# The last steps of each output group in an attention kernel: row sums added in halves ahead of the regrouping, output multiplied one unit sooner and stored two units sooner

## The chip, the core and the metric

The kernel runs on one core of a Trainium2 chip. The metric is the device time of one execution in microseconds (us). Three runs of the kernel before took 2331.0, 2331.13 and 2335.51 us; the median is 2331.13 us.

## What is computed

The input `x` has 4 images of 64 x 64 pixels with 256 channels. For each image three products with weights give q and k (128 channels) and v (256 channels). They are then read as rows of length N = 4096, with no transposition, and attention is computed over the 4096 columns:

```python
q = einsum('bwhc,cd->bwhd', x, Wq) + bq          # k, v alike
pq, pk, pv = (t.reshape(B, -1, N) for t in (q, k, v))
energy = einsum('bcn,bcm->bnm', pq, pk)
attention = softmax(energy, axis=-1)
out = einsum('bcm,bnm->bcn', pv, attention)
return gamma * out.reshape(B, W, H, C) + x
```

Everything is float32. The kernel splits each operand of a matrix product into three parts of lower precision and sums several products of them.

## The kernel before, in words

**Groups and units.** An image is worked off in 8 groups (`NG`) of 512 output columns (`NB`), a group in 16 units (`NU`) of 256 rows of the softmax sum. So there are 4 x 8 x 16 = 512 units, numbered n from 0 to 511; t = n % 16 is the unit's place in its group, and "the turn" is the unit with t = 15. A loop at the end of the fast part writes out, unit by unit, what each engine does; the order is by hand, and every engine runs its own list in order.

**One unit n** on TensorE: the first third of the energies of unit n + 2 (`cross`, L369), half of the weighted sums of unit n (`attend`, L443, into PSUM banks `a` and `b`), the rest of the energies of unit n + 2 (`energy`, L384), a piece of the next image's projections (`step`, L257 and L274), and the other half of the sums (L443). On ScalarE: a scaling of the energies in PSUM (L370), the exponential into `x` (L387), and the upper part `h` of it (L393). On VectorE, `halves(n + 1)`: the running sum `s` of the exponentials (L404), which has two halves of 512 columns, and the two lower parts `ld` (L419, L421). In the unit t = 0 there is no sum, as `x` itself becomes the new `s`. `load_k` (L356, on POOL's queue) loads the keys of unit n + 5.

**The next image** is prepared meanwhile. `step` makes q, k and v of two pixel blocks in each group: the forms of q and k on VectorE (L310) at t = 8 to 11, the forms of v on ScalarE (L155) and VectorE (L165) at t = 12 to 15. All four forms of a group, two of q and k, then two of v, use one tile tag `pf` with two buffers, so that the first form of v needs the stores of the first q/k form to have landed, and the second form of v those of the second. `store()` sends finished forms to DRAM (L338, on SP's queue): four stores for a q/k form, at t = 10 and t = 12, two for a v form, at t = 14 and t = 0. Two loads of x (L211, SP) follow at t = 13. In the last image there is nothing left to prepare. At the end of an image, from t = 3 of its last group to t = 2 of the next image's first group, `load_v` (L343, POOL) loads the new image's v, two transfers of 384 KB per unit.

**The end of a group** is `finish`, a generator. It is started at the turn, and `proceed()`, the last thing in each unit, takes each active one to its next `yield`. So the position of a `yield` says in which unit of the following group a step is issued:

| step of `finish` | queue or engine | unit of the following group |
|---|---|---|
| two stores of the halves of `s` to DRAM (`zd`, L469) | SP | the turn itself |
| eight loads of them, regrouped, into `y` (L474) | SP | 0 |
| the two parts of the output tile `o` added (L480) | VectorE | 3 |
| the sums: two reductions with a transposition between (L483 to L490), the reciprocal (L491), its store (`rd`, L492) | VectorE, SP | 6 |
| the reciprocals loaded onto all partitions (`r`, in `o`, L495) | SP | 7 |
| `o` multiplied by `r` (L498) | VectorE | 9 |
| the residual x added to `o` by an accumulating DMA (L502) | POOL | 10 |
| `o` stored to the output (L505) | SP | 13 |

`o` has one buffer. At the next turn `emptied` (L463 on ScalarE, L461 on VectorE) moves the PSUM banks into `o`, so it needs that last store to have landed, and the next group's first `attend` needs the PSUM bank that it empties. `y` lies in the buffer of the group's q. The last group of all doesn't use `finish`: `finish_last` does its end, and for it alone `whole()` in `halves` adds the two halves of `s` (L410).

Of the kernel before, what the change touches and what calls it, by code (L numbers as in the profile page):

```python
# [9 lines left out]
F32 = mybir.dt.float32  # L10
# [3 lines left out]
ALU = mybir.AluOpType  # L14
AX = mybir.AxisListType
# [5 lines left out]
def kernel(  # L21
# [36 lines left out]
    nc = tc.nc  # L58
    B, W, H, C = x.shape
    P = 128  # L60
# [21 lines left out]
    NB = 512  # L82
    NJ = NB // P
    NG = N // NB
    NU = NM // 2
    STEPS = NG * NU
# [14 lines left out]
    with ExitStack() as fast:  # L101
# [8 lines left out]
        dram = pool("dram", 2, space=DRAM)  # L110
# [4 lines left out]

        vall = qkv.tile([P, NU, 2, 3, C], F32R, tag="v", name="v")
        wf = qkv.tile([P, 2, 3, KC, C], F32R, tag="wf", name="wf")
        zd = dram.tile([B * NG, 2, P, NB], F32, tag="zd", name="zd", bufs=1)
        rd = dram.tile([B * NG, NB], F32, tag="rd", name="rd", bufs=1)
        xs4 = work.tile([P, 4, 2, XB], F32, tag="o", name="xs", bufs=1)  # L120
        raw = ppool.tile([P, 2, KC, C], F32, tag="x", name="raw")
# [223 lines left out]
        def q_tile(g, name, dtype=F32R):  # L345
            return work.tile([P, NJ, 3, P], dtype, tag=f"q{g % 2}", name=name, bufs=1)
# [49 lines left out]
        def halves(n):  # L396
            if n >= B * STEPS:
                return
            x, h = units[n]

            def summed():
                if n % NU:
                    s = now["s"]
                    nc.vector.tensor_tensor(s, s, x, ALU.add)  # L404
                else:
                    now["s"] = x

            def whole():
                s = now["sum"] = now["s"]
                nc.vector.tensor_tensor(s[:, 0, :], s[:, 0, :], s[:, 1, :], ALU.add)  # L410

            after = 0 < n < 5
            if not after:
                summed()
            if n == B * STEPS - 1:
                whole()
            ld = ppool.tile([P, 2, 2, NB], F32R, tag="ld", name=f"ld_{n}")
            l, d = ld[:, 0], ld[:, 1]
            nc.vector.tensor_tensor(l, x, h.bitcast(F32), ALU.subtract)  # L419

            nc.vector.scalar_tensor_tensor(  # L421
                d, h.bitcast(F32), 1.0 + E, x, ALU.mult, ALU.subtract
            )
            if n == 2:
                next(vs)
                next(vs, None)
            if after:
                summed()
            units[n] = h, l, d
# [35 lines left out]
        def finish(n, o, s):  # L465
            b, g = divmod(n, NG)
            r4 = rall[:, n, :]
            for i in range(2):
                nc.sync.dma_start(zd[n, i], s[:, i, :])  # L469
            yield  # L470
            y = q_tile(n, f"y_{n}", F32).rearrange("p j f a -> p (j f) a")
            for j in range(NJ):
                for i in range(2):
                    nc.sync.dma_start(  # L474
                        y[j * 32 : (j + 1) * 32, NJ * i : NJ * (i + 1)],
                        zd[n, i].rearrange("(a p) (j c) -> j p a c", p=32, j=NJ)[j],
                    )
            for _ in range(3):
                yield
            nc.vector.tensor_tensor(o[:, 0], o[:, 0], o[:, 1], ALU.add)  # L480
            for _ in range(3):
                yield
            nc.vector.tensor_reduce(  # L483
                y[:, 8].rearrange("p (f c) -> p c f", f=NJ),
                y[:, :8].rearrange("p a (c f) -> p c f a", f=NJ),
                AX.X,
                ALU.add,
            )
            nc.vector.transpose(y[:, 9], y[:, 8])
            nc.vector.tensor_reduce(r4, y[:, 9].rearrange("p (f c) -> p f c", f=NJ), AX.X, ALU.add)  # L490
            nc.vector.reciprocal(r4, r4)  # L491
            nc.sync.dma_start(rd[n, :].rearrange("(p j) -> p j", j=NJ), r4)  # L492
            yield
            r = o[:, 1, 0]
            nc.sync.dma_start(r, rd[n, :].partition_broadcast(P))  # L495
            yield
            yield
            nc.vector.tensor_tensor(  # L498
                o[:, 0], o[:, 0], r.unsqueeze(1).to_broadcast([P, 2, NB]), ALU.mult
            )  # L500
            yield
            nc.gpsimd.dma_start(o[:, 0], xg[b, g], accum_op=ALU.add)  # L502
            for _ in range(3):
                yield
            nc.sync.dma_start(og[b, g], o[:, 0])  # L505

        def inside(ok, r):
# [148 lines left out]
        for i in range(NI):  # L656
# [35 lines left out]
            if i in (7, 10):  # L692
                cross(i // 9)
            elif i in (8, 11):
                energy(i // 9)
            elif i in (9, 12):
                upper(i // 10)
            elif i == 14:
                halves(0)
# [4 lines left out]
        for n in range(B * STEPS):  # L704
# [15 lines left out]
            p = n - 2 + (n > 17)  # L720
# [16 lines left out]
            if turn:  # L737
                active.append(finish(n // NU, now["o"], now["s"]))
            if t == 0 and n and not late:
                emptied(n - 1, 1, done, vector=True)  # L740
            halves(n + 1)
            step(p, "dve")
            if final:
# [13 lines left out]
    NB = 512  # L757
    NG = N // NB
    NJ = NB // P
    NP = NM // 2  # L760
    with tc.If(nc.values_load(again[0:1, 0:1]) > 0), ExitStack() as general:
# [91 lines left out]
        for b in range(B):  # L853
# [16 lines left out]
            for g in range(NG):  # L870
                ps = []
                mx = work.tile([P, 2, NB], F32, tag="mx", name=f"gmx_{b}_{g}")
                for t in range(NP):
# [9 lines left out]
                    p = ppool.tile([P, 2, NB], F32, tag="p", name=f"gp_{b}_{g}_{t}")  # L883
# [54 lines left out]
                for s in range(2):  # L938
                    y = work.tile([P, NB], F32, tag="y", name=f"gy_{b}_{g}_{s}")
# [33 lines left out]
```

## Time and profile before

| | |
|---|---|
| median of three runs | 2331.13 us |
| the profiled execution | 2329.23 us |
| its span, first to last instruction | 2327.4 us |
| around the span | 1.8 us |
| granted TensorE clock | 0.998 |
| TensorE busy | 2309.6 us |
| VectorE busy | 2175.4 us |
| ScalarE busy | 1798.7 us |
| moved by DMA | 445.30 MB |

The span counts the time from the first to the last instruction of the profiled execution. An engine's busy time leaves out its waiting. In a row of the profile "L443 PE MATMUL a<-h,v" stands for line 443, the engine, the operation, the tile written and the tiles read; PE is TensorE, PEld its weight loads, DVE VectorE, ACT ScalarE, POOL GpSimd and SP SyncE, which only issues DMAs. In the table of waits the columns are who waited for whom, us in total, times, and the longest. In a timeline they are start, duration, what, and in brackets the idle time before it and what ended it. In a stretch of the windows view they are the stretch, its length, each engine's busy time and instructions, the granted clock, the mean busy share of the 16 DMA engines, and GB/s. In the table of DMA issues the last column is the median time from issue to landing.

### The profile page before, as it was taken

To read this page: it belongs to the slowest core of one execution; us is meant where nothing else is said; L and a number is where in the kernel's file an instruction comes from. 1 tells how busy PE (TensorE), PEld (TensorE's weight loads), DVE (VectorE), ACT (ScalarE), POOL (GpSimd) and SP (SyncE) were. 2 spreads that over 40 slices of the span, in tenths; PEclk is the share of its full clock that TensorE was granted. 3 is DMA by queue.
4 is the path that set the end of the run, shared out by engine and by line. 5 is a ranking of instruction groups with operands and counts; after the bars stand their busy time and mean duration, and the time that the engine had idled before them with its cause. 6 is when DMAs were issued, how large, how long until landed. Compare 5 with 4: busy or idle time off the path is not lost.

```text
span 2327.4 us, 31990 instructions
## 1 busy us (share of the span) xinstructions
PE 2309.6 (99%) x10758; PEld 1931.5 (83%) x10758; DVE 2175.4 (93%) x2175; ACT 1798.7 (77%) x2918; POOL 417.3 (18%) x716
## 2 busy tenths in 40 slices
PE   9999999999999999999999999999999999999998
PEld 9888888888888888888888888888888888888886
DVE  8999999999999999999999999999999999888988
ACT  7778777777777777777777777777787787888785
POOL 7111111111311111111132111111113111111110
PEclk9999999999999999999999999999999999999999
DMA  8557765577985776656798567755579755455553
GB/s 271 164 165 205 206 180 157 164 206 203 303 246 161 208 206 179 168 170 190 205 324 240 170 183 206 200 167 165 171 226 332 207 135 144 141 136 150 151 149 97
DMA packets 232190, 445.30 MB, mean 191 GB/s; under 512 B 27986, under 2 KB 109652, under 8 KB 232020
## 3 DMA queue, kind: packets, MB, share of 16 engines
q0 software_dynamic: 101120, 280.54, 45.4%
q1 hardware_dynamic: 130352, 162.38, 20.8%
q8 instruction: 88, 1.44, 0.3%
q14 instruction: 82, 0.67, 0.1%
q10 hardware_dynamic: 548, 0.26, 0.0%
HBM read 321.92 MB, written 120.39 MB: 190 GB/s over the span
## 4 chain that ended last, share of the span: by engine, by line
PE 96%; DMA 3%; DVE 0%; ACT 0%; issue 0%; POOL 0%; ACTq 0%
PE a L443 39%; PE e L384 19%; PE b L443 19%; PE e L369 10%; PE qv L257 5%; PE v L274 3%; DMA out_dram<-o 1%; PE xt L219 1%; DMA k<-kf 1%; DMA o<-in_x_dram 1%; DMA xs<-in_x_dram 0%; ACT qv L292 0%; ACT o L463 0%; DVE xf L165 0%; POOL v L343 0%
## 5 line engine op out<-in xcount | busy, mean ns | idle before, releaser
L387 ACT ACTIVATE x<-e 128x512 f32<-128x512 f32 x960 | 522.5, 596 | 323.1 <-PE e L384 323.0
L370 ACT ACTIVATE e<-e 128x512 f32<-128x512 f32 x1024 | 546.7, 571 | 134.8 <-PE e L369 134.8
L443 PE MATMUL a<-h,v 128*128 128x512 f32 x2048 | 633.7, 391 | 4.4 <-ACT o L463 4.4
L443 PE MATMUL a<-ld,v 128*128 128x512 f32 x2048 | 631.1, 389 | 0.0
L443 PE MATMUL b<-ld,v 128*128 128x512 f32 x2048 | 630.6, 389 | 0.0
L419 DVE TENSOR_TENSOR ld<-x,h 128x1024 fp32r<-128x1024 f32 x480 | 584.6, 1218 | 36.6 <-ACT h L393 23.8
L404 DVE TENSOR_TENSOR s<-s,x 128x1024 f32<-128x1024 f32 x480 | 584.2, 1217 | 35.5 <-ACT x L387 34.2
L356 POOL DMA_DIRECT2D k<-kf x512 | 272.5, 532 | 1846.7 <-PE e L384 1742.7
L421 DVE SCALAR_TENSOR_TENSOR ld<-h,x 128x1024 fp32r<-128x1024 f32 x480 | 583.9, 1216 | 0.0
L384 PE MATMUL e<-q,k 128*128 128x512 f32 x2048 | 547.7, 389 | 0.0
L393 ACT ACTIVATE h<-x 128x1024 fp32r<-128x1024 f32 x480 | 510.6, 1064 | 14.2
L443 PEld LDWEIGHTS b<-ld,v 128*128 128x128 f32 x2048 | 384.2, 188 | 80.8 <-DVE ld L421 0.6
L443 PEld LDWEIGHTS a<-ld,v 128*128 128x128 f32 x2048 | 384.3, 188 | 80.6
L384 PEld LDWEIGHTS e<-q,k 128*128 128x128 f32 x2048 | 384.2, 188 | 79.8
L443 PEld LDWEIGHTS a<-h,v 128*128 128x128 f32 x2048 | 379.4, 188 | 79.4 <-ACT o L463 5.3
L369 PE MATMUL e<-q,k 128*128 128x512 f32 x1024 | 315.8, 390 | 2.1 <-DMA k<-kf 2.1
L369 PEld LDWEIGHTS e<-q,k 128*128 128x128 f32 x1024 | 191.6, 188 | 43.1 <-ACT h L393 1.4
L310 DVE SCALAR_TENSOR_TENSOR f<-f,qv 128x512 fp32r<-128x512 f32 x128 | 85.4, 678 | 0.3
L419 DVE TENSOR_TENSOR ld<-s,h 128x1024 fp32r<-128x1024 f32 x32 | 39.3, 1227 | 46.6 <-ACT h L393 46.6
L257 PE MATMUL qv<-wf,xf 128*128 128x256 f32 x576 | 77.2, 285 | 0.4 <-DVE qv L285 0.2
L257 PEld LDWEIGHTS qv<-wf,xf 128*128 128x128 f32 x576 | 73.7, 191 | 3.5 <-issue 0.5
L165 DVE SCALAR_TENSOR_TENSOR vf<-vf,v 128x512 fp32r<-128x512 f32 x96 | 65.2, 679 | 0.3 <-ACT vf L155 0.3
(90 smaller groups left out, 1129.3 us busy)
## 6 DMA issues: line engine op xcount, KB each, us to landing
k<-kf POOLq DMA_DIRECT2D x512, 384.0 KB, 3.6
vf<-vf SPq DMA_DIRECT2D x96, 384.0 KB, 5.3
v<-vf POOLq DMA_DIRECT2D x96, 384.0 KB, 8.8
kf<-f SPq DMA_DIRECT2D x128, 192.0 KB, 3.8
qd<-f SPq DMA_DIRECT2D x124, 192.0 KB, 3.8
q<-qd POOLq DMA_DIRECT2D x31, 768.0 KB, 5.8
zd<-s SPq DMA_DIRECT2D x62, 256.0 KB, 4.9
y<-zd SPq DMA_DIRECT2D x248, 64.0 KB, 4.2
```

Source lines behind the costliest of these rows:

```text
L257: nc.tensor.matmul(to[:, s, :], left, right.rearrange("p s a -> p (s a)") if w else right, start=(f == 2 and s == k == 0), stop=(f == 1 an ...
L310: nc.vector.scalar_tensor_tensor(f[:, :, :, j, :], h.bitcast(F32), s, y, ALU.mult, op)
L356: nc.gpsimd.dma_start(t, kf[b, u % NU])
L369: nc.tensor.matmul(e, *forms(n, i, 2), start=True, stop=False, skip_group_check=True)
L370: nc.scalar.mul(e, e, -REST)
L384: nc.tensor.matmul(e, *forms(n, i, f), start=False, stop=(f == 1), skip_group_check=True)
L387: nc.scalar.activation(x[:, i, :], e, AF.Exp, scale=(1.0 + E) ** 3 / E)
L393: nc.scalar.activation(h, units[n], AF.Identity, scale=UPPER)
L404: nc.vector.tensor_tensor(s, s, x, ALU.add)
L419: nc.vector.tensor_tensor(l, x, h.bitcast(F32), ALU.subtract)
L421: nc.vector.scalar_tensor_tensor(d, h.bitcast(F32), 1.0 + E, x, ALU.mult, ALU.subtract)
L443: nc.tensor.matmul(to, vall[:, t, i, f, j * P : (j + 1) * P], units[n][f][:, i, :], start=(t == 0 and i == 0 and f != 1), stop=(t == NU - ...
```

## The change

For every group, not only the last, `whole()` adds the two halves of `s` into the first, in `halves` for t = 15, which VectorE does in the unit t = 14. `finish` then stores one half, 256 KB in place of 512, and loads it back in four transfers of 64 KB in place of eight; the first reduction goes over 4 blocks in place of 8. One `yield` is taken out ahead of the multiplication and one ahead of the store: the multiplication is issued in unit 8, the residual add in unit 9, the output store in unit 11. On SP the output store thus stands ahead of the four stores of the second q/k form (t = 12) and of the two loads of x (t = 13), where it stood behind them. On POOL the residual add stands one unit's loads earlier.

```diff
-            if n == B * STEPS - 1:
+            if n % NU == NU - 1:
                 whole()
...
-            for i in range(2):
-                nc.sync.dma_start(zd[n, i], s[:, i, :])
+            nc.sync.dma_start(zd[n], s[:, 0, :])
             yield
             y = q_tile(n, f"y_{n}", F32).rearrange("p j f a -> p (j f) a")
             for j in range(NJ):
-                for i in range(2):
-                    nc.sync.dma_start(
-                        y[j * 32 : (j + 1) * 32, NJ * i : NJ * (i + 1)],
-                        zd[n, i].rearrange("(a p) (j c) -> j p a c", p=32, j=NJ)[j],
-                    )
+                nc.sync.dma_start(
+                    y[j * 32 : (j + 1) * 32, :NJ],
+                    zd[n].rearrange("(a p) (j c) -> j p a c", p=32, j=NJ)[j],
+                )
...
             nc.vector.tensor_reduce(
-                y[:, 8].rearrange("p (f c) -> p c f", f=NJ),
-                y[:, :8].rearrange("p a (c f) -> p c f a", f=NJ),
+                y[:, 4].rearrange("p (f c) -> p c f", f=NJ),
+                y[:, :NJ].rearrange("p a (c f) -> p c f a", f=NJ),
                 AX.X,
                 ALU.add,
             )
...
             nc.sync.dma_start(r, rd[n, :].partition_broadcast(P))
-            yield
             yield
             nc.vector.tensor_tensor(
                 o[:, 0], o[:, 0], r.unsqueeze(1).to_broadcast([P, 2, NB]), ALU.mult
             )
             yield
             nc.gpsimd.dma_start(o[:, 0], xg[b, g], accum_op=ALU.add)
-            for _ in range(3):
-                yield
+            yield
+            yield
             nc.sync.dma_start(og[b, g], o[:, 0])
```

More of the change, by code (lines that the diff above doesn't have):

```diff
@@ L117 @@
         wf = qkv.tile([P, 2, 3, KC, C], F32R, tag="wf", name="wf")
-        zd = dram.tile([B * NG, 2, P, NB], F32, tag="zd", name="zd", bufs=1)
+        zd = dram.tile([B * NG, P, NB], F32, tag="zd", name="zd", bufs=1)
         rd = dram.tile([B * NG, NB], F32, tag="rd", name="rd", bufs=1)
@@ L488, in finish @@
             )
-            nc.vector.transpose(y[:, 9], y[:, 8])
-            nc.vector.tensor_reduce(r4, y[:, 9].rearrange("p (f c) -> p f c", f=NJ), AX.X, ALU.add)
+            nc.vector.transpose(y[:, 5], y[:, 4])
+            nc.vector.tensor_reduce(r4, y[:, 5].rearrange("p (f c) -> p f c", f=NJ), AX.X, ALU.add)
             nc.vector.reciprocal(r4, r4)
```

## The prediction

> **What bounds the kernel now.** I read the page's busy shares first, then the waits of TensorE, then the waits of all engines, then the chain and the timeline at the places that those named.
>
> ```profile
> PE 2309.6 (99%) x10758; PEld 1931.5 (83%) x10758; DVE 2175.4 (93%) x2175; ACT 1798.7 (77%) x2918; POOL 417.3 (18%) x716
> ```
> ```profile
> PE a L443 <- ACT o L463: 4.4, 2, 2.6
> PE e L369 <- DMA k<-kf: 2.1, 4, 1.0
> ```
> ```profile
> ACT o L463 <- DMA out_dram<-o: 5.2, 2, 3.0
> ACT vf L155 <- DMA qd<-f: 2.0, 4, 0.8
> PEld b L443 <- DVE ld L421: 0.6, 2, 0.4
> ```
>
> TensorE is busy for 2309.6 of 2327.4 us, so nothing but its idle time and its own work can move the span, and the change leaves its work alone. Inside the stream only two waits count. Twice TensorE stands still (4.4 us together) because ScalarE can't empty a PSUM bank into `o` before the store of the previous group's `o` has landed; four times (2.1 us) a key load comes late. Together 6.5 us, 0.28% of the time: that is all that can be won. VectorE is 93% busy, yet TensorE's weight loads waited for it for 0.6 us in the whole run. (About 0.2%, 4.7 us here, is what a measurement of this kernel can tell from no change.)
>
> The chain around the first of the two stalls, in order of time:
>
> ```profile
> 616.71 10.32 DMA o<-in_x_dram
> 627.04 14.54 DMA out_dram<-o
> 641.66 0.70 ACT o L463
> 642.40 1.20 PE a L443 x4
> ```
>
> So the add of the residual (issued 616.71) is late, the store starts the moment it has landed (627.04) and takes 14.54 us. Both happen at the border between two images, where 16 units load the next image's v. The busy share of the DMA engines (next to last column) shows why only there; the first row is a quiet stretch, the other three are the three borders:
>
> ```profile
> 575.00:585.00 10.00, 10.00 (x46) 8.30 (x45) 9.74 (x10) 8.28 (x13) 2.01 (x5) 1.00 0.34 87
> 612.00:635.00 23.00, 23.00 (x103) 19.06 (x102) 21.53 (x21) 17.72 (x30) 9.05 (x17) 1.00 1.12 352
> 1190.00:1212.00 22.00, 22.00 (x98) 18.22 (x98) 20.85 (x21) 17.17 (x28) 8.05 (x15) 1.00 1.13 352
> 1768.00:1790.00 22.00, 22.00 (x99) 18.22 (x98) 20.09 (x20) 17.05 (x28) 8.79 (x16) 1.00 1.12 357
> ```
>
> **The change part by part.** *VectorE.* It gains 31 half adds, and each group's first reduction reads 4 blocks in place of 8. The durations:
>
> ```profile
> L483 DVE TENSOR_REDUCE y<-y 128x128 f32<-128x1024 f32 x31 | 61.7, 1990 | 0.0
> L410 DVE TENSOR_TENSOR s<-s 128x512 f32<-128x512 f32 x1 | 0.7, 694 | 0.0
> L419 DVE TENSOR_TENSOR ld<-s,h 128x1024 fp32r<-128x1024 f32 x32 | 39.3, 1227 | 46.6 <-ACT h L393 46.6
> ```
>
> An add costs 0.69 us, 21.5 us in all; the reduction has no row at half size, so between 1.99 us (no gain) and 1.0 us (half); I take 1.0, as its time should follow what it reads: 31 us saved. The add stands ahead of the splits of unit 15, and what comes next, the splits of the new group's unit 0, sits idle for 46.6/32 = 1.46 us waiting for ScalarE's h. That idle time swallows 0.69 us. Both terms are 0 for TensorE; without that cover the add would be up to 31 x 0.69 = 21.5 us.
>
> *The multiplication, one unit sooner.* It waits for `r`. In group 3, by the timelines of VectorE and of SP, with the median landing from the table of DMA issues:
>
> ```profile
> 384.99 0.18 DVE L491 RECIPROCAL rall<-rall 128x4 f32<-128x4 f32 x1
> ...
> 392.48 1.21 DVE L404 TENSOR_TENSOR s<-s,x 128x1024 f32<-128x1024 f32 x1
> ```
> ```profile
> 385.20 0.34 SPq L492 DMA_DIRECT2D rd<-rall  x1
> 386.66 0.34 SPq L495 DMA_DIRECT2D o<-rd  x1
> ```
> ```profile
> o<-rd SPq DMA_DIRECT2D x31, 256.0 KB, 4.7
> ```
>
> VectorE reaches the new place 392.48 - 385.17 = 7.3 us after the reciprocal; `r` lands 386.66 + 4.7 = 391.4, that is 6.2 us after it. Both start together (sooner by what the reduction saves), so 1.1 us are left; about 0.5 in the last image, where the 0.6 us of a scale form isn't ahead of it. A landing that is 1 us late makes VectorE wait, and behind it stand the next unit's sum and splits; with 0.6 us of TensorE waiting for VectorE in 2327 I cost that at 0.
>
> *Bytes.* One store of 256 KB and four loads of 64 KB less per group. They lie at the turn, unit 15 and after. In 28 groups nothing waits for them. At a border they leave 0.5 MB less in front of the key loads: at 352 GB/s that is 1.5 us of the engines' time, to the good of the 2.1 us.
>
> *The add and the store sooner.* On POOL the add moves past one key load (and two v loads at a border), on SP the store moves past two loads of x and past the four stores of the second q/k form tile (call it f1). SP issues in order, and the store now waits at its head for the add. POOL's and SP's timelines at the first border:
>
> ```profile
> 611.59 1.08 POOL L343 DMA_DIRECT2D v<-vf  x2
> 615.15 0.53 POOL L356 DMA_DIRECT2D k<-kf  x1 [2.48 <-PE e L384]
> ```
> ```profile
> 621.21 0.32 SPq L338 DMA_DIRECT2D kf<-f  x1
> 621.57 0.46 SPq L338 DMA_DIRECT2D qd<-f  x1
> 622.07 0.47 SPq L338 DMA_DIRECT2D kf<-f  x1
> 622.59 0.48 SPq L338 DMA_DIRECT2D qd<-f  x1
> 624.86 1.22 SPq L211 DMA_DIRECT2D x<-in_x_dram  x2
> 627.04 0.59 SPq L505 DMA_DIRECT2D out_dram<-o  x1
> ```
>
> In a quiet group the add takes 6.7 us (below) and has landed before f1's stores are due, so nothing is held. At the first border the add can be issued after the v loads, at 612.67; with its 10.32 us it lands at 623.0, the store goes out then, and lands some 10 us before ScalarE needs `o`: **the 4.4 us go**. But f1's stores, due at 621.21, start after the store's 0.59 us, at 623.6: 2.4 us late, and behind 512 KB. Who waits for them? ScalarE, which reuses the tile for v's form. First two median landings from the table of DMA issues, then ScalarE's timeline at the three borders, with TensorE's at the second:
>
> ```profile
> o<-in_x_dram POOLq DMA_DIRECT2D x31, 512.0 KB, 6.7
> kf<-f SPq DMA_DIRECT2D x128, 192.0 KB, 3.8
> ```
> ```profile
> 633.29 0.60 ACT L155 ACTIVATE vf<-v 128x512 fp32r<-128x512 f32 x1 [0.78 <-DMA qd<-f]
> ```
> ```profile
> 1209.85 0.60 ACT L155 ACTIVATE vf<-v 128x512 fp32r<-128x512 f32 x1
> 1210.89 1.09 ACT L387 ACTIVATE s<-e 128x512 f32<-128x512 f32 x2 [0.44 <-PE e L384]
> ```
> ```profile
> 1212.50 0.61 PE L369 MATMUL e<-q,k 128*128 128x512 f32 x2
> ```
> ```profile
> 1787.61 0.60 ACT L155 ACTIVATE vf<-v 128x512 fp32r<-128x512 f32 x1 [0.54 <-DMA qd<-f]
> ```
>
> It waits for f1 already now: 0.78, 0 and 0.54 us at the three borders. Behind v's form stands the exponential, and the next TensorE matmul into `e` waits for that: at the second border there are 0.44 us of idle time and 1212.50 - 1211.98 = 0.52 us, so 1.0 us of ScalarE's lateness is free and the rest is TensorE's.
>
> How late is f1's last store? At most 2.4 us plus the store's own turn in the queue. That turn: the second load of x, issued at 625.4, landed 12.9 us later, at 638.3; the store behind it at 627.04 + 14.54 = 641.58, 3.3 us after it (the tile view of x; below it the table of DMA issues for 621 to 624 us alone):
>
> ```profile
> L211 SPq DMA_DIRECT2D x<-in_x_dram x2: 546/589/632, 624.9 to 625.4; - x2
> ...
> DMA to landing us min/median/max: 10.9/11.9/12.9
> ```
> ```profile
> kf<-f SPq DMA_DIRECT2D x2, 192.0 KB, 6.0
> ```
>
> So 5.7 at most. At least 0, if those stores were only waiting for the engines to serve the add: the first of f1's landed 6.0 us after its issue, against 3.8 in the median of all, and 2.2 us of that fell while the add was served, which will then be done. Taking those 2.2 off gives 3.5; the engines stay full of v, so I take 3.9. TensorE is then held for 0.78 + 3.9 - 1.0 = 3.7, 2.9 and 3.4 us: **10.0 us come**. A hold of 3 us at unit 15 also gives the key loads of the next units 3 us more, and with 1.5 us of traffic gone **the 2.1 us of late keys go**.
>
> [...]
>
> Sum against the profiled execution: 2329.23 - 4.4 - 2.1 + 10.0 = 2332.7 us. The median shown is 2331.13, 1.9 above that execution, so I forecast 2331.1 + 3.5 = **2334.6, say 2334.5 us**.
>
> **The rivals.**
> *The store frees more than it holds.* If f1 lands no more than some 1 us later, the 4.4 us are won and nothing new comes; of the keys' 2.1 us some return, since the stalls that are gone had given them time. For it: the 2.2 us above, and half the traffic at the turn. Against it: SP's order, fixed by the program, and an add that took 10.3 us. 2331.1 - 4.4 - 1.0 = 2325.7 us. [...]
> *f1 loses the store's whole turn* (the slower side). Place: ScalarE's v form at unit 14 of the border groups; it decides as soon as f1's last store lands more than 1.0 us after ScalarE is ready. Price at 5.7 us late: 5.5 + 4.7 + 5.2 = 15.4 - 6.5 = +8.9, 2340 us. For it: the 3.3 us between landings, and full engines. Against it: the 2.2 us.
> *`r` comes after VectorE* in most groups, because the reduction doesn't shrink or `rd` queues behind something (the change then doesn't do what it says). Place: the multiplication; it decides once `r` is over 1.1 us plus VectorE's lead late. 1 us of TensorE in each of 31 groups would be 2362 us. Against it: the 7.3 us to 6.2 us.
>
> **How the numbers follow.** Chances: forecast 0.52, store frees more 0.14, whole turn lost 0.29, late `r` 0.05. The range leaves out late `r` and the far edge of the first rival and reaches to the whole-turn price: 2326 to 2340.5. The line for slower is 2335.8, for faster 2326.5. Slower takes the whole turn, late `r` and a little of the forecast's upper side: 0.40. Faster is most of the first rival: 0.12. Within 0.2%: 0.48.
>
> **What would show it.** Right: no wait of ScalarE's L463 for the store of `o`; ScalarE's v form waiting for qd<-f three to four us at each of three borders, and TensorE's first matmul into `e` after it idle by a us less; the store ahead of f1's stores on SP's timeline, issued at the add's landing; the reduction near 1.0 us; no idle time of VectorE ahead of the multiplication outside the borders. Wrong: f1's last store landing within 11 us of its old issue time, or TensorE idle at the borders for less than 4 us in all (faster); idle time ahead of the multiplication in most groups (much slower); late keys still there, which would mean that the traffic, not the order, decides.

## The result, and the profile after

| | before | after |
|---|---|---|
| median of six runs, us | 2331.07 (2329.56 to 2335.51) | 2341.03 (2337.14 to 2343.71) |
| ratio, 95% interval | | 1.0040 (1.0029 to 1.0050) |
| profiled execution, us | 2329.23 | 2337.14 |
| span, us | 2327.4 | 2335.4 |

The change made the kernel 10 us slower in the median, 0.4%. The profiled execution of after is the fastest of its six; it stands 7.9 us above that of before. So there are two amounts to explain: 8 us that can be looked at in the trace, and 2 more in the medians. The forecast was 2334.5 us, 3.5 more than before in place of 10; the median lies half a microsecond above the stated range of 2326 to 2340.5.

The busy times of the page of after:

```profile
PE 2316.4 (99%) x10758; PEld 1935.0 (83%) x10758; DVE 2171.1 (93%) x2206; ACT 1797.1 (77%) x2918; POOL 416.3 (18%) x716
```

TensorE is busy for 6.8 us more with the same 10758 matmuls: some of its work ran slower, which idle time can't explain. VectorE has 31 instructions more and 4.3 us less. Its groups show that the half add and the shorter reduction cost nearly what was forecast, 0.69 us for 0.69 and 1.08 for 1.0 (columns: count, busy, mean ns, idle time before):

```profile
L495 DVE TENSOR_TENSOR o<-o 128x1024 f32<-128x1024 f32 x31 | 37.9, 1221 | 3.1 <-DMA o<-rd 3.1
L481 DVE TENSOR_REDUCE y<-y 128x128 f32<-128x512 f32 x31 | 33.4, 1078 | 0.0
L410 DVE TENSOR_TENSOR s<-s 128x512 f32<-128x512 f32 x32 | 22.2, 692 | 1.1
```

The waits of after, of all engines:

```profile
ACT vf L155 <- DMA qd<-f: 19.3, 6, 4.4
...
PE e L369 <- ACT s L387: 4.6, 3, 2.4
...
PE e L369 <- ACT x L387: 3.7, 3, 2.3
...
DVE o L495 <- DMA o<-rd: 3.1, 4, 1.1
```

The two rows that bounded before, ScalarE's L463 waiting for the output store and TensorE's L369 for a key load, are gone. In their place ScalarE's v form (L155) waits for the stores of the q/k forms, 19.3 us where it was 2.0, and TensorE's first matmuls into `e` wait for ScalarE's exponential behind that form: 4.6 + 3.7 = 8.3 us. There are six such waits, two at each border, where the prediction had one.

The chain at the first border, in order of time:

```profile
613.86 11.41 DMA o<-in_x_dram
...
625.28 0.59 SPq L502
...
627.57 11.28 DMA qd<-f
...
638.96 0.60 ACT vf L155
639.56 0.49 ACT s L387
...
640.10 0.99 PE e L369 x2
```

The residual add lands at 625.27, the output store (now L502) goes out then, and the last store of the second q/k form (f1) only at 627.57. SP's timeline shows the queue standing in between:

```profile
614.72 0.32 SPq L338 DMA_DIRECT2D kf<-f  x1
...
617.06 0.73 SPq L338 DMA_DIRECT2D qd<-f  x1
625.28 0.59 SPq L502 DMA_DIRECT2D out_dram<-o  x1
625.98 0.54 SPq L338 DMA_DIRECT2D kf<-f  x1
...
627.57 0.48 SPq L338 DMA_DIRECT2D qd<-f  x1
```

This place lies 1.2 us later in the span of after than in that of before (the same exponential of ScalarE starts at 611.58 and 610.36). With that taken off, f1's first store is issued 625.98 - 1.2 - 621.21 = 3.6 us later than before, where 2.4 was forecast, and its last lands 4.5 us later, where 3.9 was. But the four stores at 614.72, those of the first form (f0), are later too: the first by 1.4 us, the last by 2.4. In before the first and the last of them went out here:

```profile
612.06 0.32 SPq L338 DMA_DIRECT2D kf<-f  x1
...
613.47 0.66 SPq L338 DMA_DIRECT2D qd<-f  x1
```

Both delays reach ScalarE, as after shows:

```profile
628.58 0.60 ACT L155 ACTIVATE vf<-v 128x512 fp32r<-128x512 f32 x1 [4.37 <-DMA qd<-f]
...
638.96 0.60 ACT L155 ACTIVATE vf<-v 128x512 fp32r<-128x512 f32 x1 [2.20 <-DMA qd<-f]
```

The first of the two v forms needs f0's stores, not f1's. Here it waits longer than the second; at the other two borders the second does (2.56 and 3.31 us, then 2.93 and 3.96). And now the work that ran slower. TensorE's timeline at the second border:

```profile
1215.80 0.61 PE L443 MATMUL b<-ld,v 128*128 128x512 f32 x2
1218.11 1.24 PE L369 MATMUL e<-q,k 128*128 128x512 f32 x2 [1.70 <-ACT s L387]
1219.15 1.05 PE L443 MATMUL a<-h,v 128*128 128x512 f32 x2
...
1220.86 1.05 PE L443 MATMUL b<-ld,v 128*128 128x512 f32 x2
1221.71 1.27 PE L384 MATMUL e<-q,k 128*128 128x512 f32 x4
1222.82 0.62 PE L443 MATMUL a<-h,v 128*128 128x512 f32 x2
```

After the hold a pair of matmuls takes 1.05 us in place of 0.62, from start to start 0.86 us in place of 0.45, for 3.4 us. The windows view has the granted clock of that stretch, of the next, and of the like one at the third border (the number behind the five engines' busy times):

```profile
1218.60:1222.00 3.40, 3.40 (x9) 2.72 (x9) 2.33 (x3) 2.00 (x3) 0.00 (x0) 0.51 1.12 393
1222.00:1245.00 23.00, 23.00 (x106) 19.08 (x106) 21.12 (x22) 18.80 (x32) 7.33 (x14) 1.00 0.98 322
1798.90:1802.40 3.50, 3.50 (x9) 2.53 (x9) 2.13 (x2) 2.27 (x4) 0.00 (x0) 0.51 1.15 404
```

So two of after's six holds, of 1.70 and 2.35 us, were followed by half clock (0.51 in these rows) for 3.4 us, and half of that, 1.7 us, is lost on top of each. Taken from start to start of its matmuls (what each step takes beyond the median of the same pair of lines), TensorE lost 2.9, 2.7 and 2.6 us at the three borders in before and 4.2, 5.1 and 5.9 in after: 7.1 more before rounding. Of these 3.4 are the two halved stretches and 3.7 the holds, less the stalls that went. Another 1.2 us is lost in the first 67 us, where the clock reaches full speed at 10.4 us in place of 6.2; that loss lies between 2.6 and 5.2 us in the kernels below, with no sign of their edits, so I don't put it down to the change. 7.1 + 1.2, less 0.3 elsewhere, are the 8.0 of the span.

### The profile page after: what moved, and what is told of

Its sections match the earlier page's. It is cut to its first block, busy times and chain, and to the rows that moved or that the text cites. A ratio compares the mean times of both kernels' runs of the same rounds, so it can differ in the third digit from the quotient of the medians.

```text
span 2335.4 us, 31791 instructions
## 1 busy us (share of the span) xinstructions
PE 2316.4 (99%) x10758; PEld 1935.0 (83%) x10758; DVE 2171.1 (93%) x2206; ACT 1797.1 (77%) x2918; POOL 416.3 (18%) x716
## 4 chain that ended last, share of the span: by engine, by line
PE 96%; DMA 3%; SPq 0%; ACT 0%; issue 0%; POOL 0%; DVE 0%; POOLq 0%; ACTq 0%
PE a L443 39%; PE e L384 19%; PE b L443 19%; PE e L369 10%; PE qv L257 5%; PE v L274 2%; DMA qd<-f 2%; DMA o<-in_x_dram 1%; PE xt L219 1%; SPq L338 0%; DMA xs<-in_x_dram 0%; POOL v L343 0%; ACT vf L155 0%; SPq L502 0%; ACT qv L292 0%
## 5 line engine op out<-in xcount | busy, mean ns | idle before, releaser
L443 PE MATMUL a<-h,v 128*128 128x512 f32 x2048 | 634.4, 391 | 0.0
L443 PE MATMUL a<-ld,v 128*128 128x512 f32 x2048 | 631.9, 390 | 0.0
L443 PE MATMUL b<-ld,v 128*128 128x512 f32 x2048 | 631.6, 390 | 0.0
L443 PEld LDWEIGHTS b<-ld,v 128*128 128x128 f32 x2048 | 384.9, 188 | 80.9 <-DVE ld L421 0.6
L443 PEld LDWEIGHTS a<-ld,v 128*128 128x128 f32 x2048 | 385.0, 188 | 80.7
L443 PEld LDWEIGHTS a<-h,v 128*128 128x128 f32 x2048 | 380.3, 188 | 74.1
L369 PE MATMUL e<-q,k 128*128 128x512 f32 x1024 | 318.3, 391 | 8.3 <-ACT s L387 4.6
L369 PEld LDWEIGHTS e<-q,k 128*128 128x128 f32 x1024 | 192.1, 188 | 52.0 <-ACT s L387 6.8
```

Of the source, the lines that this page charges most:

```text
L369: nc.tensor.matmul(e, *forms(n, i, 2), start=True, stop=False, skip_group_check=True)
L443: nc.tensor.matmul(to, vall[:, t, i, f, j * P : (j + 1) * P], units[n][f][:, i, :], start=(t == 0 and i == 0 and f != 1), stop=(t == NU - ...
```

## The experiments

**Theories.** *Queue:* on SP the output store waits for the residual add ahead of f1's stores and holds them back; places decide, bytes hardly. *Add:* issuing multiplication and add one unit sooner delays f0's stores and so the first v form. *Clock:* the hold is only part of the price, the rest is the halved clock behind it. Rivals are named in each expectation. Edits are shown against after, unless another kernel is named; each kernel was compared with before on the same chip. Differences from after go by the medians of different chips; the medians of before differ by up to 0.6 us among them.

### Half the bytes alone

```diff
             nc.sync.dma_start(r, rd[n, :].partition_broadcast(P))
             yield
+            yield
...
             nc.gpsimd.dma_start(o[:, 0], xg[b, g], accum_op=ALU.add)
             yield
             yield
+            yield
             nc.sync.dma_start(og[b, g], o[:, 0])
```

> The halves are added and half the bytes moved, as in the change; multiplication, residual add and output store stay in units 9, 10 and 13. Three theories. Queue: the change is slower because the store stands ahead of the second q/k form's stores on SP. Add: it is slower because the residual add is served ahead of the first q/k form's stores, which the earlier multiplication also delays on VectorE. Regrouping: the half add or the shorter regrouping costs by itself. Queue and add both expect the two stalls on the output store to stay (4 us) and some of the 2 us of late keys to go: 2329 to 2331 us. Regrouping expects 2335 us or more.

2326.57 against 2330.47 us, ratio 0.9987 (0.9978 to 0.9996): 3.9 us faster, more than expected. So the half sum isn't what costs. ScalarE's wait for the output store fell from 5.2 to 3.6 us and the late keys from 2.1 to 1.2.

### The store back behind f1, the multiplication and the add early

```diff
             nc.gpsimd.dma_start(o[:, 0], xg[b, g], accum_op=ALU.add)
-            yield
-            yield
+            for _ in range(4):
+                yield
```

> The change with the store put back to unit 13; multiplication and add stay in units 8 and 9. Queue: the second form's stores are in time, ScalarE's second v form waits under 1 us, 2328 to 2332 us. Add: ScalarE's first v form still waits 3 to 4 us at each border and TensorE 1 to 2.5 us after it, 2333 to 2338 us.

2328.23 against 2330.47 us, 0.9988 (0.9979 to 0.9997): with the store behind f1's stores and the x loads again, 13 us of after's time are gone. The waits of this kernel:

```profile
ACT vf L155 <- DMA qd<-f: 8.0, 3, 3.0
...
PE e L369 <- ACT x L387: 1.8, 2, 0.9
```

Three waits in place of six, all of the first v form: this is the early add's share, and TensorE sees 1.8 us of it. With the store late again a part of the old stall is back, 1.3 us of TensorE in two waits. The add theory as the main cause falls; as a second one it stays.

### The store early, the multiplication and the add late

```diff
             nc.sync.dma_start(r, rd[n, :].partition_broadcast(P))
             yield
+            yield
...
             nc.gpsimd.dma_start(o[:, 0], xg[b, g], accum_op=ALU.add)
             yield
-            yield
             nc.sync.dma_start(og[b, g], o[:, 0])
```

> Half the bytes; multiplication and add back in units 9 and 10, the store left in unit 11, so that it holds SP until the later add has landed. Queue: the second form's stores go out at 627 in place of 625 at the first border, the second v form waits 5 to 7 us at each border, 2342 to 2348 us. Add: the first v form waits as little as before, so less is lost than in the change, 2333 to 2337 us.

2348.09 against 2330.47 us, 1.0067 (1.0053 to 1.0081), the top of what the queue theory expected. The waits:

```profile
ACT vf L155 <- DMA qd<-f: 24.5, 3, 8.6
...
PE e L369 <- ACT s L387: 19.7, 3, 7.0
```

Again three, but now of the second form, and longer, since the store at SP's head waits for an add that is issued a unit later. This is the queue alone. The clock is halved for 10.2, 6.8 and 6.8 us from within the three holds on, and the span's mean granted clock is 0.994.

### The store one unit later than in after, behind f1

```diff
             nc.sync.dma_start(r, rd[n, :].partition_broadcast(P))
             yield
+            yield
```

> Half the bytes; multiplication and add in units 9 and 10 as before, the store in unit 12: behind the stores of both q/k forms, ahead of the two loads of x. Queue and add both expect no new wait of ScalarE for a q/k form's stores and the output store landed 5 us sooner than before: the 4.4 us go, 2325 to 2328 us. If what counts is only how full the DMA engines are, the stall comes back as late keys or late loads of x: 2330 us.

2324.63 against 2330.47 us, 0.9972 (0.9962 to 0.9982): the best version that computes everything, 6 us faster than before and 16 faster than after. The store stands behind f1's stores and ahead of the x loads. What is left of the waits:

```profile
PE e L369 <- DMA k<-kf: 1.9, 4, 1.0
...
ACT vf L155 <- DMA qd<-f: 0.3, 1, 0.3
```

Neither wait for the output store nor hold by the forms; 1.9 us of late keys remain. No stretch of this kernel is halved, but for the start and the last 6 us.

### After without the residual add

```diff
-            nc.gpsimd.dma_start(o[:, 0], xg[b, g], accum_op=ALU.add)
```

> The change with the residual add left out (the output lacks + x), so that the store in unit 11 waits for the multiplication alone and POOL carries 512 KB less per group. It parts what the second q/k form's stores lose: the time that the store waits for the add at SP's head, or the store's own turn in the queue. If the wait for the add decides: ScalarE waits under 1.5 us for a form's stores at each border, 2325 to 2329 us. If the store's own turn decides: 2 to 3 us at each border, 2330 to 2335 us.

2321.40 against 2330.74 us, 0.9962 (0.9948 to 0.9975), below both ranges. The store keeps its place ahead of f1 on SP, with its bytes, and TensorE isn't held at the borders at all. So it is not the place that keeps f1 back, but the wait at that place. What the store's transfer costs directly ahead of f1's stores this run doesn't show: without the wait it goes out 5 us before them (615.96 and 621.01 at the first border). As this kernel doesn't move the add's bytes either, the run with the store on another queue, below, takes the wait off SP with all the bytes.

### The new places with all the bytes

Against before:

```diff
             nc.sync.dma_start(r, rd[n, :].partition_broadcast(P))
             yield
-            yield
...
             nc.gpsimd.dma_start(o[:, 0], xg[b, g], accum_op=ALU.add)
-            for _ in range(3):
-                yield
+            yield
+            yield
             nc.sync.dma_start(og[b, g], o[:, 0])
```

> The kernel before with the new places alone: multiplication in unit 8, add in 9, store in 11; both halves of the sum stored and regrouped, 512 KB. The half sum by itself gave 4 us less. If halves and places add up: 2331 + 10 + 4 = 2345 us, 2342 to 2348. If the half sum is what crowds the new order (VectorE's add ahead of unit 15's splits): 2338 us or less.

2338.65 (2333.69 to 2342.77) against 2330.74 us, 1.0040 (1.0026 to 1.0053): the ratio of after itself. I had expected it above after by what the half sum had brought alone; that was wrong. With the new places the half sum brings nothing that can be measured: ScalarE's forms wait for 18.0 us in six waits here, for 19.3 in after. What it had brought alone was shorter stalls on the store and on late keys, and this kernel has no row of either.

### TensorE held by ScalarE, in quiet groups

Against the best version above; 18 groups, far from the borders, repeat one activation that writes the same values again:

```diff
+            if n % NU == 6 and n // NU % 8 in range(1, 7) and n < 3 * STEPS:
+                for _ in range(3):
+                    nc.scalar.activation(h, units[n], AF.Identity, scale=UPPER)
```

> The version of e4, with ScalarE repeating the same upper part of one unit three more times in 18 quiet groups (3.2 us of ScalarE each, same values written), so that TensorE is held some 2 us there, far from the borders. Theory of the clock: a hold of this length costs more than itself, since in some of the 18 the granted clock is halved for 3.4 us afterwards; 18 x 2 = 36 us of holds, plus up to 1.7 us for each halving: 2324.6 + 36 + 5 to 20 = 2366 to 2381 us, with stretches of clock 0.5 in the record. Rival: the halvings belong to the full DMA engines of the borders, none here: 2361 us and a clock as in e4.

The same with four repeats:

```diff
-                for _ in range(3):
+                for _ in range(4):
```

> As e7 with four repetitions, holds of some 3 us. Theory of the clock: more of the 18 are followed by a halved clock than in e7, nearly all: 2324.6 + 54 + 25 to 31 = 2404 to 2410 us, and more than the 19 us of the added ScalarE time lies between e7 and this. Rival: 2380 us, 19 us above e7, and no halving.

Three repeats: 2383.92 against 2330.74 us, 1.0235 (1.0219 to 1.0250). Four: 2438.65, 1.0458 (1.0442 to 1.0474). Both are above the expected numbers; the holds came out longer than I had worked out, 2.4 us each in place of 2.0. TensorE's waits of the kernel with three repeats, and of the one with four:

```profile
PE e L384 <- ACT e L370: 43.3, 18, 2.4
```
```profile
PE e L384 <- ACT e L370: 62.9, 18, 3.5
```

The fourth repeat holds TensorE 19.6 us longer, but costs 54.7. The timeline of TensorE in the kernel with four (whose lines from the edit on have numbers three higher, so that L446 is L443), and the clock in the windows around it:

```profile
159.07 0.61 PE L446 MATMUL b<-ld,v 128*128 128x512 f32 x2
163.17 2.07 PE L384 MATMUL e<-q,k 128*128 128x512 f32 x4 [3.49 <-ACT e L370]
165.04 1.05 PE L446 MATMUL a<-h,v 128*128 128x512 f32 x2
```
```profile
163.20:169.20 6.00, 6.00 (x14) 4.74 (x15) 4.93 (x6) 3.58 (x6) 0.53 (x1) 0.51 0.25 66
169.20:180.00 10.80, 10.80 (x60) 9.35 (x59) 8.95 (x12) 5.65 (x10) 1.05 (x2) 1.00 0.32 71
```

Six microseconds of work at half clock are 3.0 lost. With four repeats the clock was halved after 17 of the 18 holds, in 16 of them for 6.83 us, 0.6 to 1.5 of it before the hold's end (0.87 in the one shown); with three after 5 of 18, for 3.41 us each. The expectation had counted one such stretch behind each hold; there were mostly two. 16 x 3.0 + 1.7 - 5 x 1.7 = 41 us, and with the 19.6 of the holds 61, against 58.3 between the two profiled spans. The clock theory holds: what a hold costs behind it can exceed the hold's own growth (41 us behind the holds, 19.6 in them). The DMA share is 0.25 here, so the halving needs no border.

### The store on another queue

```diff
-            nc.sync.dma_start(og[b, g], o[:, 0])
+            nc.gpsimd.dma_start(og[b, g], o[:, 0])
```

> The change with one word altered: the output store of unit 11 is issued on POOL's queue, behind the add that it waits for, in place of SP's. The same bytes are moved at nearly the same time; only the stores of the second q/k form no longer stand behind it. Queue: ScalarE's second v form waits under 1.5 us at the borders, the first as in e2 (2 to 3 us); 2327 to 2331 us. If the transfer itself is what keeps the second form's stores, whichever queue it is on: 2336 us or more. A side cost is possible: key loads behind the store on POOL, 1 to 2 us.

2328.71 against 2330.46 us, 0.9992 (0.9983 to 1.0001). One word of after changed, with the same instructions and bytes: 12 us faster than after (11 by the two ratios). On POOL's timeline the store waits for the add as it did on SP, and on SP's f1's stores go out at their time:

```profile
623.84 0.69 POOL L502 DMA_DIRECT2D out_dram<-o  x1 [2.88 <-DMA o<-in_x_dram]
624.43 0.66 POOL L356 DMA_DIRECT2D k<-kf  x1
```
```profile
620.82 0.32 SPq L338 DMA_DIRECT2D kf<-f  x1
...
622.16 0.44 SPq L338 DMA_DIRECT2D qd<-f  x1
```

This settles the queue. It isn't free on POOL: the key load stands behind the store now, and the late keys are back, while the early add's three waits of the first v form remain ("issue": the profile shows no releaser):

```profile
ACT vf L155 <- issue: 6.2, 3, 2.3
PE e L369 <- DMA k<-kf: 4.7, 6, 1.4
```

### Two checks around the best version

The multiplication and the add early, the store in the same unit as there:

```diff
             nc.gpsimd.dma_start(o[:, 0], xg[b, g], accum_op=ALU.add)
             yield
             yield
+            yield
```

> The change with the store one unit later: multiplication in unit 8, add in 9, store in 12, behind both forms' stores and ahead of the loads of x. What e2 lost against e1 (1.7 us) was the first form's wait; the store's place of e4 gave 2 us. If the two add up: 2326 to 2327 us, with ScalarE's first v form waiting 2 to 3 us at each border and the second not at all. If the add in unit 9 is free: 2324.5 us as e4.

2326.58 against 2330.46 us, 0.9985 (0.9976 to 0.9994). The first v form waits 7.4 us in three waits here, 0.3 in the best version; that prices the early add at 2326.6 - 2324.6 = 2 us, though the two intervals still overlap.

And before, with nothing but its output store one unit sooner, and all its bytes:

```diff
             nc.gpsimd.dma_start(o[:, 0], xg[b, g], accum_op=ALU.add)
-            for _ in range(3):
+            for _ in range(2):
                 yield
```

> The kernel before with one yield less ahead of the store: multiplication and add in units 9 and 10, store in 12, both halves of the sum stored and regrouped. It parts e4's 5.8 us between the half sum and the store's place. If the place alone takes the store's stall away: 2326 to 2328 us, and the half sum gives 2 to 3 us more in e4 as fewer late keys. If the half sum is what does it: 2330 us, and late keys of 4 us.

2328.70 against 2330.46 us, 0.9993 (0.9984 to 1.0002): the place alone isn't told from no change. The late keys are 4.8 us in eight waits, so the stalls on the store were exchanged for them, probably because the stalls had given the keys time. With half the bytes they are 1.9, and the kernel is 4 us faster: in that place the half sum is what pays.

## Why the prediction was right and wrong

**The path was right, by name.** The forecast said that the store stands ahead of f1's stores on SP, waits there for the add, and so holds ScalarE's v form and TensorE behind it. The one word that moved the store to POOL took 12 us off, and leaving out the add took the holds away. The store did land some 10 us before ScalarE needed `o` (634.0 and 644.0 at the first border), though the forecast worked that out from no row: with the 14.54 us of before it would have been one. Both gains it counted came: the 4.4 us of stalls and the 2.1 of late keys have no row in after.

**The step that failed is the price of a hold.** "TensorE is then held for 0.78 + 3.9 - 1.0" took a lost microsecond of TensorE to cost one microsecond. The holds less the gains did measure 3.7 us in the profiled pair, where the sum said 10.0 - 6.5 = 3.5; but the clock was halved after two of the six holds, and that is 3.4 us which the sum has no term for. The stalls of before, 2.6 us at the longest, had halved nothing, so its trace didn't show that a hold can. The holds of three and four repeats show it apart from everything else.

**That the holds' sum came out is partly luck.** Its terms were off, one way and the other:
- Where the multiplication was moved I asked only who waits for VectorE now, and put the answer at 0. But VectorE makes f0 behind the multiplication (1.22 us, and up to 1.1 of waiting for `r` in the border groups, less 0.9 that the reduction saves), so f0's stores start later and run beside the add, which itself starts one unit's loads sooner: at the first border the two into `qd` took 11.4 us each, in before 7.7 and 8.9. The first v form waits for them. The runs with the early add and the store behind f1 price this at 2 us.
- Of the 10.0 us forecast for f1's holds TensorE waited 4.6: 0.59, 1.70 and 2.35 us in place of 3.7, 2.9 and 3.4. The holds behind f0, which the sum had at nothing, were 2.31, 0.50 and 0.87 us, 3.7 in all.
- f1 came later than forecast: stores issued 3.6 us late in place of 2.4, because the add took 11.41 us in place of the 10.32 of before. Its landing, 4.5 us late, lies between the 3.9 taken and the 5.7 of the rival.
- TensorE's slack was larger, and counts once for each hold: at the first border ScalarE waited 4.37 us and TensorE 2.31, then 2.20 and 0.59, so 2.1 and 1.6 us were free where 1.0 was taken.

**The rivals.** The median lies a microsecond above the 2340 of the rival "f1 loses the store's whole turn", but its mechanism isn't what did it: f1's stores were issued 3.6 us late and landed 4.5 us late at the first border, so some 0.9 us is left for the store's own turn, where the rival took 3.3. What decided here is SP's order of issue: with the same store on POOL's queue f1's stores went out from 620.82 on, and the kernel was 12 us faster. "The store frees more than it holds" is what the kernel does once the store stands behind f1. `r` came late four times, by 3.1 us in all, and never in most groups.

**What I did not forecast and can't show** is the 2 us between the profiled pair and the medians. The five other runs of after have mean granted clocks of 0.996 and 0.997 where the profiled one has 0.998, so more halved stretches fit; there is no trace of them.

**The clock.** The two halved stretches of after last 3.413 us each in its trace, and the other stretches behind holds 3.41, 6.83 and 10.24 us: one, two and three times that. The length of a hold alone doesn't say whether one follows: half clock followed the holds of 1.70 and 2.35 us in after, and did not follow one of 2.31 us in the same kernel.

What sets these apart is in the traces: the place of the hold in steps of 3.413 us, here called windows. All changes of the clock in one trace lie whole windows apart (in after those at 1218.68 and 1798.94 lie 580.26 = 170 x 3.4133 us apart). Counted back from them, these are the windows of after in which its three longest holds lie (the first number behind the comma is TensorE's busy time):

```profile
624.76:628.17 3.41, 2.65 (x12) 1.88 (x10) 1.31 (x2) 0.00 (x0) 1.60 (x3) 1.00 1.16 404
628.17:631.59 3.42, 1.87 (x7) 1.35 (x8) 2.09 (x3) 2.98 (x5) 0.00 (x0) 1.00 1.12 395
1215.27:1218.68 3.41, 1.71 (x8) 0.87 (x6) 0.74 (x2) 1.68 (x4) 1.60 (x3) 1.00 1.13 380
1795.53:1798.94 3.41, 1.06 (x5) 0.55 (x3) 0.69 (x1) 1.37 (x3) 1.36 (x3) 1.00 1.10 397
```

The hold of 2.31 us was cut by a window's end into 0.76 and 1.55; the other two lay in one window whole, and the half clock began at its end. In the 13 traces of this case, between 67 and 2300 us, 26 windows at full clock had more than 1.95 us without a matmul, and half clock followed each; it followed none of the 8417 with less than 1.6 us, and 2 of the 12 in between. The stalls of before were cut as well (the one of 2.61 us at 641.00); no window of it had more than 1.4 us, and its clock stayed at 1.00 there: they cost only themselves. This is a count over traces, in which the ends of matmuls are modelled; no run moved a hold in its window by intent.

## What to carry to other kernels

Before a DMA is moved up on an in-order queue, ask what it waits for at its new place, and what stands behind it: a store that waits for a late transfer belongs behind every store that is ready, or on a queue whose next work can wait (here, with nothing else moved, 14 us for the first and 12 for the second: 2326.58 and 2328.71 us against 2341.03). Moving a vector operation up a unit moves everything behind it on its engine down, the first links of other chains too (2 us here, by way of f0's stores, which went out 1.4 to 2.4 us later). And when a change brings new idle time of TensorE, count each hold of 1.7 to 3.5 us with a possible 1.7 us (measured in after) to 3.0 us (with four repeats) behind it for the clock, look at the granted clock, not only at the waits, and don't conclude from one stall that cost only itself that the next will.

## What the runs showed of the hardware

- Holds of TensorE of 1.70 to 2.4 us were followed by a halved clock in some cases (2 of the 3 in after, 5 of 18 with three repeats), holds of 3.5 us in 17 of 18 with four repeats, 16 times for 6.83 us.
- All changes of the clock in one trace lay whole multiples of 3.413 us apart. In windows of that length, half clock followed each of the 26 with more than 1.95 us without a matmul, none of the 8417 with less than 1.6 and 2 of the 12 in between (13 traces, between 67 and 2300 us).
- A residual add of 512 KB took 7.2 us in the median of after and 11.41 at its first border, where the busy share of the DMA engines was 1.1; issued 4.1 us sooner at the first border than in before (with the 1.2 us of the spans taken off), it landed 3.0 us sooner.
- Half the bytes of the regrouping were worth 4 us where loads or the output store came late (2326.57 against 2330.47 us; 2324.63 against 2328.70), and nothing measurable where f1's stores stood behind the store (ratio 1.0040 with half the bytes and with all).
